# A transformer block in one program: the centre merged in place, LN1's variance and power for two groups at once, seven transposed buffers

## The chip, the core and the metric

The kernel runs on one core of a Trainium2 chip. The metric is the device time of one execution in microseconds. Before the change it is 3923.73 us, the median of three runs (3923.47 to 3927.55).

The core's engines each work through their own list of instructions in order, and wait for each other by semaphores. PE (TensorE) does matrix products and transposes, with PEld as its weight loads; DVE (VectorE), ACT (ScalarE) and POOL (GpSimd) do elementwise work; SP (SyncE) issues DMAs. POOL issues DMAs too, among them those that add to what is in the target. SBUF is the memory beside the engines, PSUM the one that PE writes to. In both, a tile is 128 partitions by so many elements.

## The reference

x has the shape (16, 128, 96, 96): 16 images, 128 channels, 96 x 96 pixels, in float32. For each image the reference computes

```
xn1 = layernorm over channels of x                       # LN1
q, k, v = xn1 wq^T, xn1 wk^T, xn1 wv^T                   # 8 heads of 16 channels
a = softmax(l2norm(q) l2norm(k)^T / 4)                   # over channels: one 16 x 16 matrix a head
x = x + (a v) wp^T
xn2 = layernorm over channels of x                       # LN2
h1 = w_in xn2                                            # 128 -> 512 channels
h2 = depthwise 3 x 3 convolution of h1 (w_dw)            # zero padding
x = x + w_out gelu(h2)                                   # 512 -> 128 channels
```

The attention is over channels, so all that it needs of the pixels is the Gram matrix of xn1. It is turned into one 128 x 128 matrix an image, which is then applied to xn1.

## The kernel before, in words

**Tiles.** An image is cut into 8 bands of 12 rows (1152 pixels), a band into 3 units of 4 rows (384 pixels). The 512 hidden channels are 4 chunks of 128. A tile of activations has channels on its partitions and pixels along the free axis. For layer norms the pixels go on the partitions: a *group* is 4 blocks of 128 pixels, transposed. An image has 18 groups.

**LN1** (`norm` with `second` false). For every group PE transposes x into a PSUM bank (`forth`, L1462), ACT copies it to a transposed buffer zT in SBUF (`copied`, L1499), DVE takes statistics of it in two instructions (`stats`, L1470), POOL forms variance plus epsilon (`variance`, L1475) and raises it to -1/2 (`power`, L1479), and POOL scales zT in place (`scaled`, L1503). Then PE adds the group to the Gram matrix (`gram`, L1510) and transposes it back (`back`, L1558), and ACT writes the result to the ring of normalised activations xn (`place`, L1564). There are 4 zT buffers. LN1 of an image runs while the image before it is in the feed-forward part. For image 0 nothing runs before it, and the scaling is done on DVE (L1483) straight from PSUM into other buffers.

**LN2** (`second` true). PE multiplies xn by the image's attention matrix (`mix`, L1412), ACT adds the bias (L1421), and a DMA from POOL adds x (L1424). Statistics, variance and power are as in LN1, but PE then only spreads the inverse deviations over the channels (L1558), and DVE multiplies (`place`, L1562) into the same ring xn.

**Feed-forward** (`conv_job`, one for a band and a chunk). PE computes h1 in pieces of 3 to 5 rows (`hidden`, L1756) and ACT copies them to a padded tile (`kept`, L1761). The nine taps of the convolution are divided among engines, scaled so that the centre tap has weight 1. ACT forms products for 2, 3 or 4 taps (`product`, L1772) into 8 buffers `pr`. POOL adds the first of these products and the unscaled centre into one common tile `merged` (`merge`, L1775; `merge_too`, L1778, adds a fourth product). DVE's first tap (L1784) reads `merged` and writes the accumulator in PSUM, further taps add to it (L1788), and the last one (L1784 again) writes h3. The second product, to which a third may have been added by a DMA (L1797), is added to h3 by an accumulating DMA (L1800), and ACT applies GELU (L1805). For some bands one chunk is computed by PE alone with nine products of the ring xn (`by_matmuls`, L1868). PE multiplies by w_out (L1904), DVE adds x (L1911), SP stores.

**The ring xn** has rows of 97 columns, of which 96 are used (`window`).

**Order.** The kernel is written with an explicit schedule. `Plan` holds every operation with an engine, an estimated duration, tokens it reads and writes, and a place. A simulation with these estimates gives each engine's list, and each list of buffers taken by several engines. `MOVES` then shifts single entries of these lists (entry number: by how much). The lists are fixed after that: each engine does its instructions in that order, whatever the real durations are. Semaphores follow from which tiles an instruction really reads and writes.

Of the kernel before, what the change touches and what calls it, by code (L numbers as in the profile page):

```python
# [17 lines left out]
UR = 4  # L18
# [18 lines left out]
QB = 1  # L37
H_BANKS = 4
TR_BANKS = 0
BK_BANKS = 0  # L40
# [6 lines left out]
ZT_BUFS = 4  # L47
BATCHES = 8
DIRECT = False
ENGINES = ("PE", "DVE", "ACT", "POOL", "SP")  # L50
IN_TURN = ("zT", "tr", "h3", "pr", "xb", "x1")
# [162 lines left out]
    PE={6: -1, 11: -1, 13: -1, 18: 0, 19: -3, 26: -1, 28: -1, 29: 7, 33: -3, 37: 3, 38: 6, 39: -4, 47: -2, 48: -2,  # L214
# [488 lines left out]
T_LAND = 1000  # L703
# [11 lines left out]
class Plan:  # L715
# [172 lines left out]
    def in_turn(self, lists):  # L888
# [40 lines left out]
        while len(sequence) < len(ops):  # L929
# [40 lines left out]
            if engine == "POOL":  # L970
                last_pool = None if queue else k
# [1017 lines left out]
```

## Time and profile before

| | before |
|---|---|
| median of 3 runs | 3923.73 us |
| profiled execution, its own time | 3923.85 us |
| its span in the profile | 3921.9 us |
| busy: PE, DVE, ACT, POOL | 3846.4, 3824.6, 3614.9, 3368.7 us |
| mean granted TensorE clock | 0.999 |

The span runs from the first to the last instruction of the profile; the execution's own time is 1.95 us longer. Rows of the profile name a line of the kernel, an engine, an operation, and the tile written and those read by their names in the program (`h` stands for the banks, the hidden tiles and h3 alike). Busy time of PE counts pipelined passes that overlap; an fp32 product is two passes. The waits name who waited for whom, with the sum in us, the number of times and the longest.

### The profile page before, as it was taken

What the parts mean: (1) busy time and instruction counts of PE and PEld (TensorE: products, weight loads), DVE (VectorE), ACT (ScalarE), POOL (GpSimd) and SP (SyncE); (2) the same over time, 40 slices, a digit from 0 to 9 for tenths busy, and PEclk for the clock granted to TensorE, in tenths of its full rate; (3) what the DMA queues carried; (4) which work ended last, traced back from release to release, by engine and by line L of the source; (5) the groups of instructions that cost most, each with busy time, mean ns of one, the idle gap of its engine ahead of it and who ended that gap; (6) DMA issues with size and microseconds to landing.
All of it is one profiled execution on the core that took longest, in us unless ns stands there. A gap on an engine that the chain in (4) does not pass through costs nothing.

```text
span 3921.9 us, 50494 instructions
## 1 busy us (share of the span) xinstructions
PE 3846.4 (98%) x16467; PEld 2477.5 (63%) x16467; DVE 3824.6 (98%) x4392; ACT 3614.9 (92%) x5478; POOL 3368.7 (86%) x3107
## 2 busy tenths in 40 slices
PE   8999999999999999999999999999999999999999
PEld 7666666666666666666666666666666666666555
DVE  7999999999999999999999999999999999999998
ACT  3999999999999999999999899999999999999986
POOL 5898899888898888989889899898998988888674
PEclk9999999999999999999999999999999999999999
DMA  3999999999999999999999999999999999999997
GB/s 93 188 205 205 191 211 205 201 203 195 214 197 209 204 192 212 203 206 203 202 206 202 195 211 203 207 197 210 207 205 201 205 208 195 207 202 188 202 188 150
DMA packets 191687, 777.36 MB, mean 198 GB/s; under 512 B 22208, under 2 KB 23616, under 8 KB 191424
## 3 DMA queue, kind: packets, MB, share of 16 engines
q0 software_dynamic: 151920, 622.33, 83.7%
q1 hardware_dynamic: 38784, 151.75, 10.6%
q8 instruction: 129, 2.11, 0.2%
q14 instruction: 134, 1.10, 0.1%
q10 hardware_dynamic: 720, 0.07, 0.0%
HBM read 148.85 MB, written 75.50 MB: 57 GB/s over the span
## 4 chain that ended last, share of the span: by engine, by line
PE 40%; DVE 9%; ACT 5%; DMA 3%; issue 2%; POOL 2%; POOLq 0%; DVEq 0%; ACTq 0%
PE h L1904 11%; PE h L1756 10%; PE h L1868 8%; DVE acc L1788 4%; PE h L1412 3%; PE h L1558 3%; PE g L1510 2%; PE h L1462 2%; ACT pr L1772 2%; DMA h<-pr 2%; DVE acc L1784 2%; DVE h L1784 1%; ACT h L1805 1%; DMA pr<-pr 1%; ACT h L1761 1%
## 5 line engine op out<-in xcount | busy, mean ns | idle before, releaser
L1772 ACT ACTIVATE pr<-h,ratio 128x1152 f32<-128x1152 f32 x1494 | 1845.2, 1268 | 14.2 <-DMA pr<-pr 2.7
L1788 DVE SCALAR_TENSOR_TENSOR acc<-h,ratio,acc 128x1152 f32<-128x1152 f32 (+1 forms) x1308 | 1810.1, 1384 | 10.9
L1775 POOL TENSOR_TENSOR merged<-pr,h 128x1152 f32<-128x1152 f32 x466 | 1212.6, 2602 | 116.6 <-DVE acc L1784 56.1
L1756 PE MATMUL h<-xn,winT 128*128 128x384 f32 (+2 forms) x2802 | 1093.3, 496 | 17.9 <-ACT h L1761 5.5
L1904 PE MATMUL h<-h,woutT 128*128 128x384 f32 x3072 | 1098.6, 487 | 3.6 <-ACT h L1761 1.4
L1868 PE MATMUL h<-xn,comp 128*128 128x380 f32 (+2 forms) x2430 | 893.5, 483 | 1.6 <-DVE st_b L1470 0.8
L1904 PEld LDWEIGHTS h<-h,woutT 128*128 128x128 f32 x3072 | 563.8, 189 | 372.6 <-ACT h L1761 16.4
L1761 ACT COPY h<-h 128x384 f32<-128x384 f32 (+2 forms) x1401 | 654.4, 492 | 110.2 <-PE h L1756 104.3
L1756 PEld LDWEIGHTS h<-xn,winT 128*128 128x128 f32 x2802 | 495.7, 189 | 348.5 <-ACT h L1761 29.7
L1784 DVE SCALAR_TENSOR_TENSOR acc<-h,ratio,merged 128x1152 f32<-128x1152 f32 x466 | 678.2, 1455 | 10.6 <-POOL merged L1775 4.7
L1784 DVE SCALAR_TENSOR_TENSOR h<-h,ratio,acc 128x1152 f32<-128x1152 f32 x467 | 655.2, 1403 | 4.5
L1805 ACT ACTIVATE h<-h,ksum 128x1152 f32<-128x1152 f32 (+1 forms) x586 | 611.0, 1069 | 27.0 <-DMA h<-pr 26.1
L1800 POOL DMA_DIRECT2D h<-pr x466 | 477.1, 1032 | 165.1 <-DVE h L1784 18.5
L1868 PEld LDWEIGHTS h<-xn,comp 128*128 128x128 f32 x2430 | 431.4, 190 | 234.2 <-issue 16.0
L1797 POOL DMA_DIRECT2D pr<-pr x466 | 469.6, 1025 | 73.7 <-ACT pr L1772 50.9
L1479 POOL TENSOR_TENSOR ve_a<-ve_a,mhalf 128x4 f32<-128x4 f32 x288 | 356.7, 1241 | 10.9
L1479 POOL TENSOR_TENSOR ve_b<-ve_b,mhalf 128x4 f32<-128x4 f32 x288 | 339.8, 1195 | 10.0
L1503 POOL TENSOR_TENSOR zT<-zT,ve_a 128x512 f32<-128x512 f32 x270 | 339.5, 1260 | 7.0
L1462 PE MATMUL h<-ident,x 128*128 128x128 f32 x2244 | 320.9, 275 | 9.3 <-DVE st_b L1470 2.3
L1462 PEld LDWEIGHTS h<-ident,x 128*128 128x128 f32 x2244 | 263.8, 141 | 101.3 <-issue 38.9
L1412 PE MATMUL h<-xn,mwT 128*128 128x384 f32 x768 | 288.8, 491 | 8.2 <-ACT x L1421 3.5
L1510 PEld LDWEIGHTS g<-zT 128*128 128x128 f32 x2160 | 271.9, 191 | 36.5 <-issue 3.0
(187 smaller groups left out, 3858.7 us busy)
## 6 DMA issues: line engine op xcount, KB each, us to landing
pr<-pr POOLq DMA_DIRECT2D x466, 576.0 KB, 7.2
h<-pr POOLq DMA_DIRECT2D x466, 576.0 KB, 7.8
x<-in_x_dram SPq DMA_DIRECT2D x128, 576.0 KB, 6.8
out_dram<-x SPq DMA_DIRECT2D x127, 576.0 KB, 4.9
x<-in_x_dram POOLq DMA_DIRECT2D x123, 576.0 KB, 8.3
out_dram<-x SPq DMA_DIRECT2D x3, 192.0 KB, 1.9
h<-in_L_conv_w_in_dram SPq DMA_DIRECT2D x1, 256.0 KB, 3.4
h<-in_L_conv_w_out_dram SPq DMA_DIRECT2D x1, 256.0 KB, 3.6
```

The lines of the kernel that those rows point to most:

```text
L1462: nc.tensor.transpose(d["pT", q][:, k, :], xt[:, j * P : (j + 1) * P], ident)
L1479: nc.gpsimd.tensor_tensor(rstd, rstd, mhalf, ALU.pow)
L1756: nc.tensor.matmul(rows(ph), lhsT=winT[:, n, :], rhs=window(xn, r0 + r, e - r, 1), start=True, stop=True)
L1761: nc.scalar.copy(window(h1_, r, e - r, 1), rows(d.pop(("ph", r))))
L1772: nc.scalar.activation(to, shifted(t), AF.Copy, scale=ratio[:, n, t : t + 1])
L1775: nc.gpsimd.tensor_tensor(merged, d["pr", dma_taps[0]], shifted(UNIT), ALU.add)
L1784: nc.vector.scalar_tensor_tensor(to, shifted(t), ratio[:, n, t : t + 1], also, ALU.mult, ALU.add)
L1788: nc.vector.scalar_tensor_tensor(to, shifted(t)[:, lo:hi, cut], ratio[:, n, t : t + 1], to, ALU.mult, ALU.add)
L1800: nc.gpsimd.dma_start(out=h3_of(g, n), in_=d["pr", dma_taps[1]], accum_op=ALU.add)
L1805: nc.scalar.activation(h3, h3, AF.Gelu, bias=ksum[:, z, n : n + 1])
L1868: nc.tensor.matmul(d["pc"][:, lo:hi, cut], lhsT=comp[:, t, :], rhs=window(xn, r0 + dy, UR, dx)[:, lo:hi, cut], start=(t == order[0]), stop ...
L1904: nc.tensor.matmul(rows(d["po"]), lhsT=woutT[:, n, :], rhs=h3s[g, n][:, s * UR : (s + 1) * UR, :], start=(k == 0), stop=(k == NCH - 1),)
```

## The change

1. `merge` and `merge_too` write into the buffer of the first product instead of the common tile `merged`, which is dropped. The first tap reads that buffer.
2. LN1 of images 1 to 15 takes variance and power of two groups in one instruction each (`QA = 2`): the statistics of both groups go into one tile, and both groups' scalings come behind that power. Image 0 (`QB_0`) and LN2 (`QB`) stay at one group.
3. There are 7 zT buffers instead of 4.
4. The ring xn has rows of 96 columns, without the spare one. Rows are then read and written as one run; the nine products of `by_matmuls` cut their columns out of it as before.
5. Estimates in the planner are altered (PE's rate, small POOL operations, a lag behind a DMA issue on POOL), a place's turn for buffers no longer contains its shift, options that were off are removed, and the lists in `MOVES` are rewritten, with lists for the buffers `x1` and `xb` besides.

```diff
-QB = 1
+QA, QB, QB_0 = 2, 1, 1
-ZT_BUFS = 4
+ZT_BUFS = 7
...
-IN_TURN = ("zT", "tr", "h3", "pr", "xb", "x1")
+IN_TURN = ("zT", "h3", "pr", "xb", "x1")
...
 MOVES = dict(
-    PE={6: -1, 11: -1, 13: -1, 18: 0, 19: -3,
...
+    PE={3: 0, 5: -5, 10: -1, 11: 2, 16: -1, 19: -2,
...
-PE_RATE, SPARE = 0.989, 75
+PE_RATE, SPARE, LAG, ISSUED = 1.013, 75, 300, 250
...
-T_POWER = 360 + 165 * QT * QB
-T_SMALL = 190
+T_POWER = 360, 165
+T_SMALL = 275
...
-    xn = pad.tile([P, (RING + 2) * WP + 2], F32, name="xn")
+    xn = pad.tile([P, (RING + 2) * W], F32, name="xn")
...
-    merged = h1p.tile([P, BR, W], F32, name="merged")
...
+    def pixels(r, n):
+        return xn[:, r * W : (r + n) * W]
+
+    def xn_rows(r, lo, hi, dx, cut):
+        return rows(pixels(r + lo, hi - lo))[:, :, cut.start + dx - 1 : cut.stop + dx - 1]
...
-        return window(xn, ring_of(i, u * UR) + 1, UR, 1)
+        return pixels(ring_of(i, u * UR) + 1, UR)
...
-        return Place(place + (AT[of] + SHIFTS.get(max(0, int(place // STRETCH)), {}).get(of, 0)), RANK.get(kind, 0))
+        shift = SHIFTS.get(max(0, int(place // STRETCH)), {}).get(of, 0)
+        return Place(place + AT[of], shift + RANK.get(kind, 0))
...
+        qb = (QB if second else QA) if i else QB_0
...
-                    d["st"] = small.tile([P, QB * QT // 2, 6], F32, tag="st", name=f"st_{name}_{m}")
+                    d["st"] = small.tile([P, qb * QT // 2, 6], F32, tag="st", name=f"st_{name}_{m}")
...
-                ve = d["ve"] = small.tile([P, QB * QT], F32, tag="ve", name=f"ve_{name}_{m}")
+                ve = d["ve"] = small.tile([P, qb * QT], F32, tag="ve", name=f"ve_{name}_{m}")
...
-                nc.gpsimd.tensor_tensor(rstd, rstd, mhalf, ALU.pow)
+                nc.gpsimd.tensor_tensor(rstd, rstd, mhalf[:, : qb * QT], ALU.pow)
...
-                nc.gpsimd.tensor_tensor(z, z, d["rstd"].unsqueeze(2).to_broadcast([P, QT, P]), ALU.mult)
+                nc.gpsimd.tensor_tensor(z, z, d["rstd"][:, q % qb * QT : (q % qb + 1) * QT].unsqueeze(2).to_broadcast([P, QT, P]), ALU.mult)
...
-                    nc.vector.tensor_tensor(interior(i, u), rows(x_unit(xbs, i, u)), rows(d["pB"]), ALU.mult)
+                    nc.vector.tensor_tensor(interior(i, u), x_unit(xbs, i, u), d["pB"], ALU.mult)
...
-                rows(ph), lhsT=winT[:, n, :], rhs=window(xn, r0 + r, e - r, 1), start=True, stop=True
+                rows(ph), lhsT=winT[:, n, :], rhs=rows(pixels(r0 + r, e - r)), start=True, stop=True
...
-            nc.gpsimd.tensor_tensor(merged, d["pr", dma_taps[0]], shifted(UNIT), ALU.add)
+            to = d["pr", dma_taps[0]]
+            nc.gpsimd.tensor_tensor(to, to, shifted(UNIT), ALU.add)
...
-            nc.gpsimd.tensor_tensor(merged, merged, d["pr", dma_taps[3]], ALU.add)
+            to = d["pr", dma_taps[0]]
+            nc.gpsimd.tensor_tensor(to, to, d["pr", dma_taps[3]], ALU.add)
...
-                also = acc if t == left[-1] else merged if dma_taps else shifted(UNIT)
+                also = acc if t == left[-1] else d["pr", dma_taps[0]] if dma_taps else shifted(UNIT)
...
-            pool(T_MERGE, at("merge", j), merge, [*h1, pr[0]], [("merged", 0)], True)
+            pool(T_MERGE, at("merge", j), merge, h1, [pr[0], ("merged", 0)], True)
...
-            r = [*h1, ("merged", 0)] if k == 0 and dma_taps else h1
+            r = [*h1, pr[0], ("merged", 0)] if k == 0 and dma_taps else h1
```

More of the change, by code (lines that the diff above doesn't have):

```diff
@@ L706, with __new__ @@
 class Place(float):
-    def __new__(cls, turn, rank):
-        place = float.__new__(cls, turn + rank)
+    def __new__(cls, turn, late):
+        place = float.__new__(cls, turn + late)
         place.turn = turn
@@ L971, in in_turn @@
                 last_pool = None if queue else k
+                lag = 2 if queue else lag if time < free_at["POOL"] + 40 else 0
+                if queue:
+                    ns -= ISSUED
+                elif lag:
+                    result += LAG * lag / 2
+                    lag -= 1
             begin[k], done[k], own[k], free_at[engine] = time, time + result, time + mine, time + ns
@@ L1042, in tile_restormer_block @@
     banks = [p_h.tile([P, 4 * P], F32, name=f"h_{k}") for k in range(H_BANKS)]
-    trs_ = [p_h.tile([P, 4 * P], F32, name=f"tr_{k}") for k in range(TR_BANKS)]
-    bks = [p_h.tile([P, 4 * P], F32, name=f"bk_{k}") for k in range(BK_BANKS)]
     acc_banks = p_acc.tile([P, ACC_BANKS * 4 * P], F32, name="acc")
@@ L1057, in tile_restormer_block @@
     nc.gpsimd.memset(ones, 1.0)
-    mhalf = const.tile([P, QB * QT], F32, name="mhalf")
+    mhalf = const.tile([P, max(QA, QB) * QT], F32, name="mhalf")
     nc.gpsimd.memset(mhalf, -0.5)
@@ L1165, in t_mm @@
     def t_mm(n):
-        return 2 * max(111, 0.849 * n)
+        return 2 * max(110, 0.841 * n)
     def t_dve(n):
@@ L1411, in mix @@
                 pm = d["pm"] = bank((name, u), UT)
-                nc.tensor.matmul(rows(pm), lhsT=mats[i][0], rhs=interior(i, u), start=True, stop=True)
+                nc.tensor.matmul(rows(pm), lhsT=mats[i][0], rhs=rows(interior(i, u)), start=True, stop=True)
                 if (i, b) not in xbs:
@@ L1436, in x2, with batch @@
                 add(at("add_x", s, u), add_x, [], xb)
-        def pixels(s, m):
+        def batch(s, m):
             d = {}
-            qs = range(m * QB, (m + 1) * QB)
+            qs = range(m * qb, (m + 1) * qb)
             early = i == 0 and (not second or m < EARLY)
-            key_ = "h" if not TR_BANKS else "tr"
             def tr_of(q):
-                return ("acc", q % BANKS_0) if in_acc(q) else (key_, (name, q, "tr"))
+                return ("acc", q % BANKS_0) if in_acc(q) else ("h", (name, q, "tr"))
             def in_acc(q):
@@ L1450, in pixels @@
             apart = i == 0 and not second
-            from_psum = second or DIRECT or apart
+            from_psum = second or apart
             def forth(q):
@@ L1456, in forth @@
                 else:
-                    of = bank((name, q, "tr")) if key_ == "h" else trs_[plan.slot["tr", (name, q, "tr")]]
+                    of = bank((name, q, "tr"))
                 d["pT", q] = of.rearrange("p (t c) -> p t c", c=P)
@@ L1524, in pixels @@
                     to = [tr] if second or apart else [tr, both[0]]
-                    pe(112 * QT, at("forth" + ab, s, m * QB * QT // TPU), lambda q=q: forth(q), [xtok(u) for u in units], to)
+                    pe(110 * QT, at("forth" + ab, s, m * qb * QT // TPU), lambda q=q: forth(q), [xtok(u) for u in units], to)
                     continue
-                pe(112 * QT, at("forth" + ab, s, m * QB * QT // TPU), lambda q=q: forth(q), [xtok(u) for u in units], [tr, both[0]])
-                act(t_copy(QT * P), at("copied" + ab, s, m * QB * QT // TPU), lambda q=q: copied(q), [tr], both)
-            for j in range(QB * QT // 2):
+                pe(110 * QT, at("forth" + ab, s, m * qb * QT // TPU), lambda q=q: forth(q), [xtok(u) for u in units], [tr, both[0]])
+                act(t_copy(QT * P), at("copied" + ab, s, m * qb * QT // TPU), lambda q=q: copied(q), [tr], both)
+            for j in range(qb * QT // 2):
                 of = trs[2 * j // QT] if from_psum else (*zt_of(qs[2 * j // QT]), 0)
-                dve(341, at("stats" + ab, s, m * QB * QT // TPU), lambda j=j: stats(j), [of], [bt])
-            pool(T_SMALL, at("variance" + ab, s, m * QB * QT // TPU), variance, [], [bt])
-            pool(T_POWER, at("power" + ab, s, m * QB * QT // TPU), power, [], [bt])
+                dve(341, at("stats" + ab, s, m * qb * QT // TPU), lambda j=j: stats(j), [of], [bt])
+            pool(T_SMALL, at("variance" + ab, s, m * qb * QT // TPU), variance, [], [bt])
+            pool(T_POWER[0] + T_POWER[1] * qb * QT, at("power" + ab, s, m * qb * QT // TPU), power, [], [bt])
             for h, q in enumerate(qs if not second else ()):
@@ L1550, in back @@
             def back():
-                d["pB"] = bks[plan.slot["bk", (name, u)]][:, :UT] if BK_BANKS else bank((name, u, "back"), UT)
+                d["pB"] = bank((name, u, "back"), UT)
                 for j in range(TPU):
@@ L1561, in place @@
                 if second:
-                    nc.vector.tensor_tensor(interior(i, u), rows(x_unit(xbs, i, u)), rows(d["pB"]), ALU.mult)
+                    nc.vector.tensor_tensor(interior(i, u), x_unit(xbs, i, u), d["pB"], ALU.mult)
                 else:
-                    nc.scalar.copy(interior(i, u), rows(d["pB"]))
+                    nc.scalar.copy(interior(i, u), d["pB"])
             def place_row(r, row):
-                nc.scalar.copy(window(xn, r, 1, 1), interior(i, u)[:, row : row + 1, :])
+                nc.scalar.copy(pixels(r, 1), interior(i, u)[:, row * W : (row + 1) * W])
             copies = []
@@ L1574, in channels @@
                 copies.append((0, UR - 1, -1))
-            pb = ("bk", (name, u)) if BK_BANKS else ("h", (name, u, "back"))
+            pb = ("h", (name, u, "back"))
             quads = {(u * TPU + j) // QT: None for j in range(TPU)}
             if second:
-                ms = {q // QB: None for q in quads}
-                pe(112 * TPU, at("back" + ab, s, u), back, [("batch", (name, m)) for m in ms], [pb])
+                ms = {q // qb: None for q in quads}
+                pe(110 * TPU, at("back" + ab, s, u), back, [("batch", (name, m)) for m in ms], [pb])
                 dve(t_dve(UT), at("place" + ab, s, u), place, [pb, xtok(u)], [z_unit(i, u)])
             else:
-                pe(112 * TPU, at("back" + ab, s, u), back, [(*zt_of(q), k) for q in quads for k in range(2)], [pb, z_unit(i, u)])
+                pe(110 * TPU, at("back" + ab, s, u), back, [(*zt_of(q), k) for q in quads for k in range(2)], [pb, z_unit(i, u)])
                 act(t_copy(UT), at("place" + ab, s, u), place, [pb], [z_unit(i, u)])
@@ L1594, in norm @@
         u = 0
-        for m in range(NU * TPU // (QB * QT)):
-            pixels(place_of(m * QB * QT), m)
-            while u < NU and (u + 1) * TPU <= (m + 1) * QB * QT:
+        for m in range(NU * TPU // (qb * QT)):
+            batch(place_of(m * qb * QT), m)
+            while u < NU and (u + 1) * TPU <= (m + 1) * qb * QT:
                 channels(place_of(u * TPU), u)
@@ L1833, in conv_job @@
         if dma_taps:
-            pool(T_MERGE, at("merge", j), merge, [*h1, pr[0]], [("merged", 0)], True)
+            pool(T_MERGE, at("merge", j), merge, h1, [pr[0], ("merged", 0)], True)
             if len(dma_taps) > 3:
-                pool(T_MERGE, at("merge", j), merge_too, [pr[3]], [("merged", 0)], True)
+                pool(T_MERGE, at("merge", j), merge_too, pr[3:], [pr[0], ("merged", 0)], True)
         for k, t in enumerate(left):
-            r = [*h1, ("merged", 0)] if k == 0 and dma_taps else h1
+            r = [*h1, pr[0], ("merged", 0)] if k == 0 and dma_taps else h1
             w = all_acc if k < len(left) - 1 else h3
@@ L1868, in product @@
             nc.tensor.matmul(
-                d["pc"][:, lo:hi, cut], lhsT=comp[:, t, :], rhs=window(xn, r0 + dy, UR, dx)[:, lo:hi, cut],
+                d["pc"][:, lo:hi, cut], lhsT=comp[:, t, :], rhs=xn_rows(r0 + dy, lo, hi, dx, cut),
                 start=(t == order[0]), stop=(t == order[-1]),
```

40 lines of the change are left out of this document (20 added, 20 removed), and 1589 rows, old and new, of tables (ACT, DVE, PE, POOL).

## The prediction

> **What bounds the kernel now.** I read the page first, for busy shares and for the chain of work that ended last.
>
> ```profile
> span 3921.9 us, 50494 instructions
> ...
> PE 3846.4 (98%) x16467; PEld 2477.5 (63%) x16467; DVE 3824.6 (98%) x4392; ACT 3614.9 (92%) x5478; POOL 3368.7 (86%) x3107
> ...
> PE 40%; DVE 9%; ACT 5%; DMA 3%; issue 2%; POOL 2%; POOLq 0%; DVEq 0%; ACTq 0%
> PE h L1904 11%; PE h L1756 10%; PE h L1868 8%; DVE acc L1788 4%; PE h L1412 3%; PE h L1558 3%; PE g L1510 2%; PE h L1462 2%; ACT pr L1772 2%; DMA h<-pr 2%; DVE acc L1784 2%; DVE h L1784 1%; ACT h L1805 1%; DMA pr<-pr 1%; ACT h L1761 1%
> ```
>
> PE and DVE stand at 98% together, and the chain passes between them. PE's 98% is soft: its busy time counts overlapped passes. DVE's is hard, since its instructions barely overlap. So the second view is busy time by stage.
>
> ```profile
> 0.00:100.00 100.00, 89.97 (x582) 72.50 (x583) 72.02 (x187) 34.48 (x70) 55.88 (x112) 1.00 0.32 93
> 100.00:3880.00 3780.00, 3718.09 (x15767) 2382.37 (x15767) 3726.91 (x4183) 3563.19 (x5377) 3307.80 (x2992) 1.00 0.97 202
> 3880.00:3922.00 42.00, 38.33 (x122) 22.63 (x120) 25.70 (x24) 17.25 (x33) 5.06 (x4) 0.99 0.47 111
> ```
>
> The columns after the length are PE, PEld, DVE, ACT and POOL. Between 100 and 3880 us DVE is idle for 3780 - 3726.9 = 53 us (1.4%), ACT for 217 us and POOL for 472 us. The start and the end leave DVE idle for 28 and 16 us. The DMA engines are at 0.97 there, but the change neither adds nor removes a transfer, so they can't be relieved by it. This sets the scale: if the change shortens no DVE instruction, what it can win in the long stage is those 53 us. The third view is what DVE waits for in that stage.
>
> ```profile
> DVE x L1911 <- PE h L1904: 6.2, 13, 1.4
> DVE xn L1562 <- PE h L1558: 5.5, 11, 1.1
> DVE st_b L1470 <- PE h L1462: 4.3, 9, 1.1
> DVE acc L1784 <- POOL merged L1778: 3.7, 7, 1.2
> DVE acc L1784 <- POOL merged L1775: 3.3, 7, 1.4
> ```
>
> PE's three rows make 16 us, the merges on POOL 7 us. Nothing else is above 2.5 us. A lighter POOL by itself can therefore give back 7 us through DVE and no more.
>
> **The merge in place.** L1775 and L1778 wrote one common buffer, so the next merge had to wait until the first tap (L1784) had read it. Now each merge writes the product's own buffer, and that wait is gone.
>
> ```profile
> POOL merged L1775 <- DVE acc L1784: 56.1, 64, 2.7
> POOL merged L1775 <- ACT pr L1772: 48.6, 48, 5.1
> ```
>
> That is 56 us of POOL idle, out of 472, on an engine that has room. What is late next is the product on ACT (48.6 us already). What queues behind a merge on POOL are the variances, the powers and the issues of the accumulating DMAs. I credit no POOL time as such, only the 7 us for which DVE waited for merges; bounds 0 and -7, and I take **-7**, because the merges lose both this wait and the work below from ahead of them. The price is that the first product's buffer stays taken until the tap has read it, not until the merge is done. There are eight such buffers, and ACT waited for a merge to free one for very little:
>
> ```profile
>   POOL merged L1775: 2.2, 5
> ```
>
> A buffer freed one tap later costs ACT at most that again and a little more, and the 217 us of ACT idle cover it: **0**. If that cover is gone, each late product makes its accumulating DMA, and then its GELU, late by a tap, 1.4 us.
>
> The wait had also kept something apart. A merge and a first tap both read two operands from SBUF, and they don't run side by side:
>
> ```profile
> L1784 DVE SCALAR_TENSOR_TENSOR acc<-h,ratio,merged x466: 1396/1412/3682, 87.8 to 3884.7; 128x1152 f32<-128x1152 f32 x156
> ```
>
> ```profile
> 1746.96 2.63 POOL L1503 TENSOR_TENSOR zT<-zT,ve_a 128x512 f32<-128x512 f32 x2
> ...
> 1747.14 3.68 DVE L1784 SCALAR_TENSOR_TENSOR acc<-h,ratio,merged 128x1152 f32<-128x1152 f32 x1
> ```
>
> The tap that met two scalings in a row took 3.68 us where the median is 1.41. With a mean of 1455 ns (its row stands below), all such blocking costs 466 x (1.455 - 1.412) = 20 us now. Without the old wait, a merge whose product is there could begin ahead of the preceding tap and hold it up. I went through the 64 waits in the order of time: in nine of them POOL came free before that tap had begun. First, one in the middle with its tap, and last:
>
> ```profile
> 714.16 2.43 POOL L1775 TENSOR_TENSOR merged<-pr,h 128x1152 f32<-128x1152 f32 x1 [2.21 <-DVE acc L1784]
> ...
> 1757.20 1.41 DVE L1784 SCALAR_TENSOR_TENSOR acc<-h,ratio,merged 128x1152 f32<-128x1152 f32 x1
> 1758.76 2.42 POOL L1775 TENSOR_TENSOR merged<-pr,h 128x1152 f32<-128x1152 f32 x1 [2.23 <-DVE acc L1784]
> ...
> 3794.17 2.42 POOL L1775 TENSOR_TENSOR merged<-pr,h 128x1152 f32<-128x1152 f32 x1 [2.70 <-DVE acc L1784]
> ```
>
> In the middle one POOL was free at 1758.76 - 2.23 = 1756.53, the tap began at 1757.20. A merge begun at 1756.53 would end at 1758.95 and push the tap by 1.75 us. Over the nine that makes 9 x 1.75 = 16 us, if every product had been there. In the other 55 the tap was already running, and the merge would wait for it as before. I take **+3**, some two cases, since the work ahead of the merges moves too; the bounds are -20 (all blocking gone) and +16.
>
> [...]
>
> **Variance and power for two groups at once.** For images 1 to 15 that is 15 x 18 / 2 = 135 pairs; image 0 and LN2 stay at one group.
>
> ```profile
> L1479 POOL TENSOR_TENSOR ve_a<-ve_a,mhalf x288: 997/1032/2935, 8.5 to 3570.0; 128x4 f32<-128x4 f32 x144
> ...
> L1679 POOL TENSOR_TENSOR rn<-n,mhalf x16: 707/710/713, 54.2 to 3592.9; 128x2 f32<-128x2 f32 x16
> ...
> L1475 POOL TENSOR_SCALAR ve_a<-st_a x288: 184/396/2281, 8.2 to 3567.0; 128x4 f32<-128x4 f32 x144
> ```
>
> The power of eight columns isn't in the trace. Two and four columns give (1032 - 710) / 2 = 161 ns a column, so eight take an estimated 1032 + 4 x 161 = 1676 ns against 2 x 1032: 0.39 us less a pair. One variance less saves up to 0.40 us. Together 135 x 0.79 = 106 us of POOL, which comes to nothing directly: POOL's 472 idle us hide it, and its share in the merges is in the -7.
>
> Against it stands a longer way for the first group of a pair. Its scaling (L1503), Gram matmuls (L1510) and transposes back (L1558) now wait for the second group's statistics, and PE has other passes queued behind them. The trace shows how near that wait is today:
>
> ```profile
> PEld h L1558 <- POOL zT L1503: 5.2, 11, 1.3
> ...
> PEld g L1510 <- POOL zT L1503: 1.9, 4, 0.8
> ```
>
> So 270 scalings made PE wait 7 us, and LN1 of an image runs a whole image ahead of its use. Seven transposed buffers in place of four hold the two to three more groups under way. I take **0**. The bounds are -7 (these waits go) and +20: one in ten of the 135 pairs late by the whole 1.68 us power makes 135 / 10 x 1.68 = 23, less some that is covered.
>
> **The activations without a padding column.** The diff also stores xn with 96 columns a row, not 97. Matmuls that read whole rows then read one run of 384. The trace has both kinds of reading:
>
> ```profile
> L1904 PE MATMUL h<-h,woutT 128*128 128x384 f32 x3072 | 1098.6, 487 | 3.6 <-ACT h L1761 1.4 <-DVE st_b L1470 1.2 <-DVE xn L1562 0.6
> L1756 PE MATMUL h<-xn,winT 128*128 128x384 f32 x2184 | 849.4, 492 | 12.9 <-ACT h L1761 3.2 <-DVE x L1911 2.4 <-ACT xn L1564 2.0
> L1784 DVE SCALAR_TENSOR_TENSOR acc<-h,ratio,merged 128x1152 f32<-128x1152 f32 x466 | 678.2, 1455 | 10.6 <-POOL merged L1775 4.7 <-POOL merged L1778 3.7
> L1868 PE MATMUL h<-xn,comp 128*128 128x384 f32 x788 | 322.4, 491 | 1.6 <-DVE st_b L1470 0.8 <-ACT h L1761 0.5
> L1412 PE MATMUL h<-xn,mwT 128*128 128x384 f32 x768 | 288.8, 491 | 8.2 <-ACT x L1421 3.5 <-DVE st_b L1470 3.2 <-ACT d L1720 0.5
> ...
> L1911 DVE TENSOR_TENSOR x<-h,x 128x384 f32<-128x384 f32 x384 | 210.5, 550 | 20.3 <-PE h L1904 18.8 <-ACT h L1752 0.7 <-ACT h L1805 0.3
> L1562 DVE TENSOR_TENSOR xn<-x,h 128x384 f32<-128x384 f32 x384 | 209.9, 548 | 11.1 <-PE h L1558 5.5 <-issue 2.4 <-ACT x L1421 1.5
> ```
>
> L1904 reads 384 in one run at 487 ns; the reads of xn in rows take 4 to 5 ns more. So PE saves 2184 x 5 + 788 x 4 + 768 x 4 = 17 us. How much of that is on the path follows from the chain, where a run of passes shows their true pace, and from the group of all L1756:
>
> ```profile
> 3904.79 13.56 PE h L1904 x42
> ...
> L1756 PE MATMUL h<-xn,winT 128*128 128x384 f32 (+2 forms) x2802 | 1093.3, 496 | 17.9 <-ACT h L1761 5.5
> ```
>
> A pass takes 13.56 / 42 = 323 ns, so L1756's 10% of the chain, 392 us, is 1214 of its 2802 passes, 43%. 17 x 0.43 gives **-7**; bounds 0 and -17. On DVE the write to xn gains nothing: 548 ns with the padding against 550 for L1911, which writes one run.
>
> **The order lists.** Every engine's list of moves is rewritten along with these edits. I can't cost this from a row; where it goes wrong is a rival. For image 0, at the start, the work is the same: 0, within 10 us either way, out of DVE's 28 idle us there.
>
> **The sum.** -7 + 3 + 0 - 7 = -11 us. The profiled execution took 3923.85 us (1.95 us outside its span), the median of the runs is 3923.73: 3923.85 - 11 = 3912.9, and 3913 against that median is -0.3%. A measurement of this kernel tells about 0.2%, 8 us, from no change.
>
> **The rivals.**
>
> *Hidden anyway.* DVE's busy time stays at 3825 us, and the gaps that PE and POOL no longer cause are filled by the next wait in line. For it: no DVE instruction gets shorter, and the chain's changes of engine are frequent. Against it: DVE's waits are named and two of the changes bear on them. Time: 3923, within 8 us.
>
> [...] At the first tap, POOL's two-operand instructions start ahead of it more often: merges without the old wait, and scalings that now come in pairs, as in the row at 1746.96, where the price was 3.68 - 1.41 = 2.27 us. For it: the nine cases, and 135 pairs released by one power. Against it: only some 20 of 466 taps are held up today. The other terms make -14 us, so from 14 / 2.27, some six more taps than today, it eats the gain. All nine merges (16 us) and eight taps met by a pair (18 us) give 3923.85 - 14 + 34 = 3944.
>
> *The order doesn't fit the pairs.* PE comes to Gram or back passes ahead of the pair's scalings, and everything behind on PE waits. If 20 pairs hit that for 1.68 us and DVE follows, 34 - 11 = +23: 3947. Against it: 7 us of such waits today.
>
> *More than the terms.* The new order also closes half of DVE's idle time in the long stage, 53 us less the 7 that are in the sum: 3923.85 - 11 - 23 = 3890.
>
> **How the numbers follow.** Forecast 0.43, hidden anyway 0.23, ports 0.12, order 0.14, more 0.08. Faster by over 0.2%: three quarters of the forecast's 0.43 (its term for PE may stay hidden), a tenth of the second and the last case: 0.32 + 0.02 + 0.08 = 0.42. Slower: the two slow cases but for a sixth, and 0.03 of the second: 0.22 + 0.03 = 0.25. The rest, 0.33, is no change. The forecast's own range is 3900 to 3923. For 8 times in 10 the low end takes in the better order, 3890, and the high end both slow ones, 3948.
>
> **What would show it.** Right: the wait of the merge for the tap (56.1 us) gone; the waits of DVE for merges near 0; the power with eight columns near 1.68 us, 135 of them; L1756 at 487 ns; DVE's busy time within 5 us of 3825. Wrong: first taps with a mean well above 1455 ns (ports), PE waiting for zT by more than 20 us (order), or DVE's busy time down by more than 10 us, which no term here gives.

## The result and the profile after

The changed kernel takes 3964.95 us (median of four runs, 3961.66 to 3970.0) against 3924.68 us for the kernel before, measured beside it: a ratio of 1.0103, with a 95% interval of 1.0085 to 1.012. It is 40 us slower. The prediction had 3913, with a range of 3890 to 3948.

The profiled execution took 3970.0 us, the longest of the four. First its page: the span, the busy times and the shares of the chain that ended last.

```profile
span 3968.2 us, 49765 instructions
...
PE 3856.2 (97%) x16467; PEld 2490.3 (63%) x16467; DVE 3861.1 (97%) x4392; ACT 3617.0 (91%) x5478; POOL 3295.3 (83%) x2840
...
PE 31%; DVE 9%; ACT 4%; DMA 4%; POOL 2%; issue 2%; DVEq 0%; POOLq 0%; ACTq 0%
```

POOL has become 73 us lighter (3368.7 before), as the pairs were meant to make it; 106 us were forecast. But DVE has become 36.5 us busier (3824.6 before) with the same 4392 instructions. Its idle time, span less busy, went only from 97.3 to 107.1 us. Of the 46.3 us between the two spans, 36.5 lie inside DVE's instructions and 9.8 in the waits between them. The group rows say which instructions. Columns: count, busy time and mean ns of one, idle time before them and what ended it.

```profile
L2457 DVE SCALAR_TENSOR_TENSOR acc<-h,ratio,pr 128x1152 f32<-128x1152 f32 x466 | 714.1, 1532 | 5.9 <-POOL pr L2451 2.7 <-POOL pr L2447 2.0
L2447 POOL TENSOR_TENSOR pr<-pr,h 128x1152 f32<-128x1152 f32 x466 | 1270.7, 2727 | 66.5 <-ACT pr L2443 65.7
```

The first taps took 678.2 us before and 714.1 now: 35.9 of the 36.5 us. The wait of the merge for the tap (56.1 us before) is gone, and the merges themselves went from a mean of 2602 ns to 2727.

DVE's waits in the whole span, with us in total, times and the longest:

```profile
DVE x L2584 <- PE h L2577: 20.6, 17, 4.3
DVE xn L2233 <- PE h L2229: 18.7, 29, 2.6
...
DVE acc L2457 <- POOL pr L2451: 2.7, 3, 1.1
DVE acc L2457 <- POOL pr L2447: 2.0, 6, 0.5
```

DVE waits 4.7 us for merges, against 4.7 + 3.7 = 8.4 us before in the same view. Its wait in LN2 for PE's spreading of the inverse deviations (L2229; 5.5 us before) is 18.7.

What a long tap looks like is seen in the timeline (start, length, engine, line; in brackets the idle time before it). This one is the longest of the trace:

```profile
778.55 0.92 POOL L2470 DMA_DIRECT2D pr<-pr  x1
778.67 7.45 DVE L2457 SCALAR_TENSOR_TENSOR acc<-h,ratio,pr 128x1152 f32<-128x1152 f32 x1
...
779.23 1.32 POOL L2174 TENSOR_TENSOR zT<-zT,ve_a 128x512 f32<-128x512 f32 x1
780.24 0.47 POOL L2146 TENSOR_SCALAR ve_b<-st_b 128x4 f32<-128x4 f32 x1
780.38 1.17 POOL L2473 DMA_DIRECT2D h<-pr  x1
780.98 1.47 POOL L2470 DMA_DIRECT2D pr<-pr  x1
781.54 3.35 POOL L2447 TENSOR_TENSOR pr<-pr,h 128x1152 f32<-128x1152 f32 x1
783.92 3.06 POOL L2150 TENSOR_TENSOR ve_b<-ve_b,mhalf 128x4 f32<-128x4 f32 x1
786.04 0.54 DVE L2233 TENSOR_TENSOR xn<-x,h 128x384 f32<-128x384 f32 x1
...
786.63 0.90 PE L2229 MATMUL h<-ident,ve_b 128*128 128x128 f32 x3 [5.56 <-DVE xn L2233]
```

The median of the first taps was 1.41 us before. This one was held for 6 us by a scaling, a variance and the next merge, which passed it, with two DMA issues between them. The old wait made that merge impossible: it would have stood behind the tap. The power behind the merge took 3.06 us instead of 1.0 and ended at 786.98, 0.86 us after the tap, which fits a wait for the tap. PE stood still for 5.6 us meanwhile. The windows show what followed; the columns after the length are PE, PEld, DVE, ACT, POOL, granted clock, DMA share, GB/s.

```profile
781.00:786.60 5.60, 0.08 (x1) 0.00 (x0) 5.60 (x3) 1.84 (x2) 5.60 (x4) 0.78 1.07 262
786.60:791.00 4.40, 4.37 (x13) 3.17 (x14) 4.40 (x6) 0.85 (x3) 0.39 (x1) 0.50 0.95 189
791.00:800.00 9.00, 9.00 (x46) 6.22 (x46) 8.20 (x11) 8.16 (x13) 3.99 (x5) 1.00 0.42 82
```

After the gap PE ran at half its clock. In the whole trace eleven first taps took over 3.6 us (one before). From 150 us to 10 us before the end, nine stretches at half clock add up to 47.8 us. The kernel before has none there, but two just ahead, at 105 and 119 us, of 3.4 us each. Stretches at half clock are counted between these bounds from here on.

Last, the rows for the pairs: the powers (minimum, median and maximum ns), PE's waits for a scaling, and ACT's waits for a product buffer.

```profile
L2150 POOL TENSOR_TENSOR ve_a<-ve_a,mhalf x153: 1006/1662/3092, 10.5 to 3609.1; 128x8 f32<-128x8 f32 x135, 128x4 f32<-128x4 f32 x18
```

```profile
PEld g L2181 <- POOL zT L2174: 3.7, 7, 0.9
...
PE g L2181 <- POOL zT L2174: 0.5, 2, 0.3
```

```profile
ACT pr L2443 <- DMA h<-pr: 8.0, 10, 2.5
ACT pr L2443 <- DMA pr<-pr: 6.9, 9, 2.1
ACT pr L2443 <- DVE acc L2457: 3.0, 1, 3.0
```

A power of eight columns takes 1.66 us. PE's wait for scalings at the Gram matmuls is 4.2 us, and 0.8 at the transposes back, so the pairs' order fits. ACT waits 18.6 us for buffers with the smaller rows, where it was 5.5.

### The profile page after: what moved, and what is told of

Its sections match the earlier page's. It is cut to its first block, busy times and chain, and to the rows that moved or that the text cites. A ratio compares the mean times of both kernels' runs of the same rounds, so it can differ in the third digit from the quotient of the medians.

```text
span 3968.2 us, 49765 instructions
## 1 busy us (share of the span) xinstructions
PE 3856.2 (97%) x16467; PEld 2490.3 (63%) x16467; DVE 3861.1 (97%) x4392; ACT 3617.0 (91%) x5478; POOL 3295.3 (83%) x2840
## 4 chain that ended last, share of the span: by engine, by line
PE 31%; DVE 9%; ACT 4%; DMA 4%; POOL 2%; issue 2%; DVEq 0%; POOLq 0%; ACTq 0%
PE h L2577 9%; PE h L2427 8%; PE h L2541 7%; DVE acc L2461 4%; DMA h<-pr 2%; PE h L2084 2%; PE g L2181 2%; DVE acc L2457 2%; PE h L2229 2%; PE h L2133 2%; ACT pr L2443 2%; DVE h L2457 2%; ACT h L2478 1%; POOL pr L2447 1%; DMA pr<-pr 1%
## 5 line engine op out<-in xcount | busy, mean ns | idle before, releaser
L2447 POOL TENSOR_TENSOR pr<-pr,h 128x1152 f32<-128x1152 f32 x466 | 1270.7, 2727 | 66.5 <-ACT pr L2443 65.7
L2427 PE MATMUL h<-xn,winT 128*128 128x384 f32 (+2 forms) x2802 | 1112.7, 498 | 27.3 <-DVE xn L2233 7.1
L2577 PE MATMUL h<-h,woutT 128*128 128x384 f32 x3072 | 1123.0, 488 | 7.1 <-DVE x L2584 2.0
L2457 DVE SCALAR_TENSOR_TENSOR acc<-h,ratio,pr 128x1152 f32<-128x1152 f32 x466 | 714.1, 1532 | 5.9 <-POOL pr L2451 2.7
L2473 POOL DMA_DIRECT2D h<-pr x466 | 459.6, 988 | 283.5 <-PE h L2577 49.4
L2133 PE MATMUL h<-ident,x 128*128 128x128 f32 x2244 | 337.3, 277 | 27.1 <-DMA x<-in_x_dram 8.2
L2150 POOL TENSOR_TENSOR ve_b<-ve_b,mhalf 128x4 f32<-128x4 f32 x288 | 349.3, 1230 | 9.3
L2174 POOL TENSOR_TENSOR zT<-zT,ve_a 128x512 f32<-128x512 f32 x270 | 352.6, 1338 | 2.9
L2084 PE MATMUL h<-xn,mwT 128*128 128x384 f32 x768 | 302.5, 494 | 15.7 <-ACT x L2093 6.0
L2181 PE MATMUL g<-zT 128*128 128x129 f32 x2160 | 286.3, 276 | 0.5 <-POOL zT L2174 0.5
```

Source lines behind the costliest of these rows:

```text
L2133: nc.tensor.transpose(d["pT", q][:, k, :], xt[:, j * P : (j + 1) * P], ident)
L2181: nc.tensor.matmul(grams[i][:, : P + 1], lhsT=zt[:, :P], rhs=zt, start=(q == 0 and k == 0), stop=(q == NU * TPU // QT - 1 and k == QT - 1),)
L2427: nc.tensor.matmul(rows(ph), lhsT=winT[:, n, :], rhs=rows(pixels(r0 + r, e - r)), start=True, stop=True)
L2447: nc.gpsimd.tensor_tensor(to, to, shifted(UNIT), ALU.add)
L2457: nc.vector.scalar_tensor_tensor(to, shifted(t), ratio[:, n, t : t + 1], also, ALU.mult, ALU.add)
L2577: nc.tensor.matmul(rows(d["po"]), lhsT=woutT[:, n, :], rhs=h3s[g, n][:, s * UR : (s + 1) * UR, :], start=(k == 0), stop=(k == NCH - 1),)
```

## The experiments

The leading theory was that without the old wait merges start ahead of the previous first tap and hold it up. The rivals: the loss lies in the new order, in the pairs, or in the product buffers held one tap longer. Each edit keeps the order that its base kernel gives to every engine (the added repetitions and split instructions stand where the single ones stood). In code, "..." stands for lines that are left out. Medians in us, ratios against the kernel before measured beside it:

| kernel | median us (runs) | ratio [95%] |
|---|---|---|
| after_wait | 3928.59 (10) | 1.0009 [0.9998, 1.002] |
| before_inplace | 4047.18 (4) | 1.0311 [1.0296, 1.0327] |
| before_inplace_wait | 3963.15 (4) | 1.0092 [1.0079, 1.0106] |
| before_ring96 | 3921.12 (10) | 0.9993 [0.9984, 1.0003] |
| after_split | 3995.84 (4) | 1.0183 [1.0168, 1.0198] |
| after_wait_split | 3949.01 (4) | 1.0058 [1.0045, 1.0072] |
| before_lump | 4076.13 (4) | 1.0377 [1.0361, 1.0393] |
| before_spread | 4034.51 (4) | 1.0275 [1.0261, 1.0289] |
| after_gate | 3938.74 (5) | 1.003 [1.0017, 1.0044] |
| after_wait_gate | 3923.91 (11) | 0.9991 [0.9982, 1.0] |
| before_gate | 3916.23 (7) | 0.9976 [0.9965, 0.9987] |
| ring96_gate | 3914.25 (8) | 0.9972 [0.9961, 0.9982] |

### The wait put back into the changed kernel

The merge stays in place, and waits for the first tap ahead of it:

```
-            nc.gpsimd.tensor_tensor(to, to, shifted(UNIT), ALU.add)
+            m = nc.gpsimd.tensor_tensor(to, to, shifted(UNIT), ALU.add)
+            if first_tap:
+                tc.add_manual_dep(m.ins, first_tap[-1].ins.name, ...)
...
+                if t == left[0]:
+                    first_tap.append(v)      # v: the tap on DVE
...
```

> The changed kernel with one thing put back: each merge waits again until the first tap of the job before it has ended (an explicit dependency; the merge still writes in place, every engine's order is the same). Theory A, the missing wait: merges that start ahead of a held-up first tap cost the 41 us. Then the first taps above 3.6 us go, their mean falls from 1532 ns to about 1455, half-clock stretches of PE in the middle of the run fall from 9 to 0 or 1, and the time is 3915 to 3930. Theory B, the order: the other order of the lists costs the 41 us by itself. Then the taps get shorter but the time stays above 3950. Theory C, pairs of scalings on POOL in a row hold up the taps: the mean of the first taps stays above 1490 ns and the time is 3940 to 3960.

The page, the tap's group and the merge's wait for it:

```profile
span 3932.5 us, 50062 instructions
...
PE 3841.3 (98%) x16467; PEld 2479.9 (63%) x16467; DVE 3826.6 (97%) x4392; ACT 3615.6 (92%) x5478; POOL 3276.8 (83%) x2840
```

```profile
L2459 DVE SCALAR_TENSOR_TENSOR acc<-h,ratio,pr 128x1152 f32<-128x1152 f32 x466 | 681.3, 1462 | 5.9 <-POOL pr L2453 2.8 <-POOL pr L2447 2.0
```

```profile
POOL pr L2447 <- DVE acc L2459: 46.5, 71, 3.4
```

One wait on POOL takes the median from 3964.95 to 3928.59, 36 of the 40 us. In the spans it is 35.7 us, and the first taps give 714.1 - 681.3 = 32.8 of them. DVE's idle time is 105.9 us against 107.1, so it hardly changed. The half clock fell from 47.8 to 13.7 us along with it, in three stretches where none or one had been expected, but the idle times show that it was a companion of the loss and not its size. The 4 us that are left can't be told from nothing: the interval of the ratio holds 1.

### The merge in place alone, and with its wait

In the kernel before, only the merge is put in place, with the product's buffer kept until the tap has read it; then the same dependency is added.

```
-            nc.gpsimd.tensor_tensor(merged, d["pr", dma_taps[0]], shifted(UNIT), ALU.add)
+            to = d["pr", dma_taps[0]]
+            nc.gpsimd.tensor_tensor(to, to, shifted(UNIT), ALU.add)
...
```

> The kernel before with the merge in place alone; every engine's order is that of before, the buffers of the first product are held until the tap has read them. Theory A: slower, since the nine merges that POOL could start early now do so, and those behind a held-up tap as well: first taps of 4 us and more appear, mean above 1480 ns, time 3935 to 3965, with half-clock stretches. Theory B: within 8 us of before, 3917 to 3932. The term of the prediction for it alone: -7 + 3 = -4, 3920.

> The kernel before with the merge in place, and each merge waiting for the first tap before it as the common tile had made it wait; the order of before. Theory A (the missing wait alone costs the 123 us of the merge in place): 3917 to 3932, no first tap above 4 us. Rival (the first product's buffers, held until the tap has read them, hold up ACT): it stays well above 3960, with ACT waiting for the tap at the products.

Without the wait, the page, the tap and ACT's waits:

```profile
PE 3886.8 (96%) x16467; PEld 2495.6 (62%) x16467; DVE 3911.3 (97%) x4392; ACT 3619.2 (89%) x5478; POOL 3385.5 (84%) x3107
```

```profile
L1788 DVE SCALAR_TENSOR_TENSOR acc<-h,ratio,pr 128x1152 f32<-128x1152 f32 x466 | 759.8, 1631 | 8.9 <-POOL pr L1778 3.8 <-POOL pr L1782 3.0
```

```profile
ACT pr L1774 <- DVE acc L1788: 36.4, 22, 5.7
ACT pr L1774 <- DMA pr<-pr: 23.0, 22, 3.1
ACT pr L1774 <- DMA h<-pr: 21.7, 22, 2.9
```

With it:

```profile
PE 3857.7 (97%) x16467; PEld 2479.3 (63%) x16467; DVE 3832.0 (97%) x4392; ACT 3617.7 (91%) x5478; POOL 3369.6 (85%) x3107
```

```profile
L1790 DVE SCALAR_TENSOR_TENSOR acc<-h,ratio,pr 128x1152 f32<-128x1152 f32 x466 | 679.4, 1458 | 9.5 <-POOL pr L1778 3.8 <-POOL pr L1784 3.3
```

```profile
ACT pr L1774 <- DMA h<-pr: 27.7, 28, 3.9
ACT pr L1774 <- DMA pr<-pr: 26.0, 24, 3.8
```

In the old order the edit by itself costs 123 us, three times what the whole change costs; the expectation had ended at 3965 us. The wait is worth 4047.18 - 3963.15 = 84 us. In the spans (4045.4 and 3965.1 us) it is 80.3, and the first taps give 759.8 - 679.4 = 80.4: all of it. Some 36 us stay when the taps are as short as before (0.0092 of 3924). In the profiled executions, 43 us apart, 36 are DVE's idle time, 133.1 us against 97.3. What the edit still changes is that the buffer stays held, and ACT's waits for a product buffer, some 65 us with the smaller rows against 5.5, are its trace. Only 4.6 us of them are waits for the tap itself; most are for the DMAs that read the other products. That held buffers are the cause is therefore argued from these waits and not shown; no run gave the kernel a ninth buffer.

### The pairs split again

Variance and power are done for each of the two groups in an instruction of its own, where the pair's stood; without and with the merges' wait.

```
...
-                nc.gpsimd.tensor_tensor(rstd, rstd, mhalf[:, : qb * QT], ALU.pow)
+                for k in range(0, qb * QT, QT):
+                    nc.gpsimd.tensor_tensor(rstd[:, k : k + QT], rstd[:, k : k + QT], mhalf[:, :QT], ALU.pow)
```

> The changed kernel with variance and power of a pair as two instructions each of four columns, at the same place in the same order. POOL gets some 100 us of work back. If POOL's lighter load is worth something, the time rises above 3975; if it is covered, it stays within 8 us of 3965. Theory C (a power that releases two scalings at once): no gain, since the scalings still stand one behind the other.

> The changed kernel with the merges' wait, and variance and power of a pair as two instructions each. This prices the part of the change that takes two groups at once, once the missing wait is out of the picture. If a POOL lighter by some 100 us is covered, as the prediction had it: within 8 us of 3929. If it is worth as much as without the wait: 3960.

After_split's taps, then after_wait_split's busy times and its waits for merges:

```profile
L2459 DVE SCALAR_TENSOR_TENSOR acc<-h,ratio,pr 128x1152 f32<-128x1152 f32 x466 | 733.0, 1573 | 12.3 <-POOL pr L2449 6.4 <-POOL pr L2453 4.7
```

```profile
PE 3848.2 (97%) x16467; PEld 2482.2 (63%) x16467; DVE 3830.0 (97%) x4392; ACT 3617.0 (92%) x5478; POOL 3358.2 (85%) x3110
```

```profile
DVE acc L2461 <- POOL pr L2449: 7.3, 12, 1.9
...
DVE acc L2461 <- POOL pr L2455: 6.0, 8, 1.5
```

The pairs are a gain, not the loss: 3949.01 - 3928.59 = 20 us with the wait, and 3995.84 - 3964.95 = 31 us without. With the wait most of it is DVE's idle time (3948.1 - 3830.0 = 118.1 us against 105.9): DVE waits 13.3 us for merges where the pairs leave 4.8. Without the wait most of it is in the taps (733.0 against 714.1), which fits a longer row of POOL instructions holding them longer. The wait is worth 47 us here. The 20 us lie between the two values that had been expected, none and 31.

### The ring of 96 columns alone

```
-    xn = pad.tile([P, (RING + 2) * WP + 2], F32, name="xn")
+    xn = pad.tile([P, (RING + 2) * W], F32, name="xn")
...
```

> The kernel before with the ring of 96 columns alone, the same order. The term of the prediction: matmuls that read whole rows fall from 492 to 487 ns, and the time by 7 us, 3917. The rival, hidden: passes get shorter, the time stays within 4 us of before. A third: passes stay at 492 ns, since the row break was not what cost the 5 ns.

```profile
L1910 PE MATMUL h<-h,woutT 128*128 128x384 f32 x3072 | 1101.4, 488 | 3.7 <-ACT h L1767 1.5 <-DVE st_b L1476 1.0 <-DVE xn L1568 0.7
L1762 PE MATMUL h<-xn,winT 128*128 128x384 f32 x2184 | 849.1, 493 | 15.9 <-DVE x L1917 4.2 <-ACT h L1767 3.8 <-ACT xn L1570 2.1
```

The passes over whole rows take 493 ns with rows that lie end to end, and took 492 with the padding. The premise was wrong: the 5 ns against L1910's passes don't come from the padding. What they come from stays open. The time is 3 us lower, and the interval of the ratio, 0.9984 to 1.0003, holds 1.

### A stall in lumps or spread out

To price the half clock of PE that comes with long taps, the kernel before repeats a last tap (the same value is written again): seven times in every 30th job, 96 extra taps in 16 lumps, or twice in every fifth job, 94 extra.

```
+                for _ in range(7 if t == left[-1] and j % 30 == 15 else 1):    # before_lump
+                for _ in range(2 if t == left[-1] and j % 5 == 0 else 1):      # before_spread
...
```

> The kernel before with the last tap of a job done seven times instead of once in every 30th job: 96 further instructions of 1.40 us on DVE, in 16 lumps of 8.4 us (the same value is written again). If PE's clock falls to half behind a gap in its work, and this is worth something, half-clock stretches appear in most of the 16 places and the time rises by more than the 96 x 1.34 = 129 us that DVE needs for them: 4075 to 4110. [...]

> The same with single repetitions in every fifth job: 94 further instructions on DVE, none next to another. DVE sets the pace in the long stage, so nearly all of 94 x 1.34 = 126 us is added: 4035 to 4055, with no more than three half-clock stretches. Less, if DVE's gaps take up some.

Span and mean granted clock, lumps first:

```profile
core 0: 4075.7 us, clock 0.982
```

```profile
core 0: 4032.5 us, clock 0.998
```

Two taps more, and 41.6 us between the medians, or 2.6 us a lump. Both times lie at the low edge of what was expected, the second one 0.5 us below it. Behind every one of the 16 lumps PE ran at half clock; with one stretch more these add up to 139.9 us, and the spread taps leave two stretches, 6.8 us. So a lump costs some 2.6 us more than the same taps spread out, its stretch at half clock included; that a lump of 8 us is also absorbed worse by the buffers isn't separated from it.

### Scalings that wait for the tap

The scaling can hold a tap as a merge does: the tap at 1747.14 in the kernel before took 3.68 us, against a median of 1.41. Here each scaling waits for the first tap ahead of it in the program, in four kernels: the changed one with merges free (after_gate), the changed one with their wait (after_wait_gate), the one before (before_gate), and the one before with the ring of 96 (ring96_gate).

```
-                nc.gpsimd.tensor_tensor(z, z, d["rstd"]..., ALU.mult)
+                m = nc.gpsimd.tensor_tensor(z, z, d["rstd"]..., ALU.mult)
+                if first_tap:
+                    tc.add_manual_dep(m.ins, first_tap[-1].ins.name, ...)
```

> The changed kernel with the scalings waiting for the last first tap before them in the program, but the merges free, as the change has them. If a scaling ahead of the tap is what begins each long hold-up, and the merge only lengthens it: first taps above 3.6 us fall from 11 to 3 or fewer, time 3930 to 3945. If merges alone begin them, behind the issue of a DMA: half of the 11 stay, time above 3950.

> The changed kernel with the merges waiting for the first tap before them, and the scalings too; the order of the change. What is left of held-up taps there is 21 us. If the scalings cause it, as with the kernel before: mean of the first taps below 1435 ns, and 8 to 15 us less than with the merges' wait alone: 3913 to 3921. If pairs of scalings now come late for PE: no gain, and PE waiting for zT by more than 20 us.

> The kernel before with the scalings' wait alone, ring of 97 columns. If the gain of the ring and the wait together (0.9972) is the wait's: 3912 to 3918, ratio 0.997 to 0.9985. If it took both: above 3920.

> The kernel before with the ring of 96 columns, and with each scaling of LN1 on POOL waiting for the last first tap that stands before it in the program. What holds up the 19 taps above 1.5 us are such scalings; where tap and scaling stand in that order, the tap now goes first. If most do: the mean of the first taps falls from 1453 to below 1430 ns, and the time by 5 to 15 us against the ring alone, 3906 to 3916. If the scalings stand before the taps in the program: no change, 3921.

Before_gate's first taps; then ring96_gate's busy times, its first taps, and the price of the wait on POOL:

```profile
L1786 DVE SCALAR_TENSOR_TENSOR acc<-h,ratio,merged 128x1152 f32<-128x1152 f32 x466 | 666.2, 1430 | 10.7 <-POOL merged L1777 5.1 <-POOL merged L1780 3.2
```

```profile
PE 3839.5 (98%) x16467; PEld 2488.2 (64%) x16467; DVE 3808.8 (97%) x4392; ACT 3613.1 (92%) x5478; POOL 3358.1 (86%) x3107
```

```profile
L1792 DVE SCALAR_TENSOR_TENSOR acc<-h,ratio,merged 128x1152 f32<-128x1152 f32 x466 | 664.2, 1425 | 11.9 <-POOL merged L1783 5.9 <-POOL merged L1786 3.5
```

```profile
POOL zT L1509 <- DVE acc L1792: 16.9, 28, 1.4
```

With merges free, waiting scalings win back 26 of the 36 us (3964.95 to 3938.74), and five of the eleven long taps remain, which is neither of the two outcomes that were expected: it fits hold-ups that begin with either kind of POOL work, and six of the eleven are gone where scalings can't begin one. With both waits the changed kernel is at 3923.91, no different from the kernel before, with a mean of the first taps of 1440 ns; both just miss what was expected. In the kernel before, the scalings' wait alone gives a ratio of 0.9976: the blocking that was there all along, 20 us by the prediction's count, goes down to 466 x (1.430 - 1.416) = 6.5 us (the tap's mean and median in before_gate). Ring96_gate has the lowest median of all, 3914.25 us, ratio 0.9972 with an interval of 0.9961 to 0.9982: 0.3% below the kernel before, at a price of 17 us of idle time on POOL. Whether the ring adds to the wait isn't told: the two intervals overlap.

## Why the prediction was wrong

**The missing wait (+3): the right mechanism, the size wrong.** This is the step that failed. It measured +36 us in the changed kernel, and +84 in the old order. That is 33 of the 52 us between forecast and result. The prediction named the mechanism and took two of nine cases, at most 16 us; its rival of taps held up more often, with a chance of 0.12, reached 34 us with 17 blocked taps, and put the time at 3944. (By the trace the cases are eight, 14 us: in the others POOL came free at least 0.1 us after the tap had begun.) The cases were found by walking through the trace of before and asking where POOL stood free ahead of the tap. But that trace was made under the wait: POOL was paced by it. Without it POOL runs ahead: merges recorded as starting more than 0.1 us before the previous tap had ended number 113 in the changed kernel and 103 in before_inplace, none where the wait is. Those that began over 1.5 us before its end are few (12 and 27). And blocking isn't one instruction for one tap: a tap that a scaling holds is passed by the next merge, as at 778.67, for 6 us instead of 2.3. The row at 1746.96 already had this in it: the tap began 0.18 us into the first of two scalings, and was held through the second one as well. The price of a case was wrong as well as the number.

The prediction's count let a merge hold a tap until its own end and no longer, 1.75 us in its example. The full block fits the trace of the changed kernel, and goes both ways: the tap at 778.67 ended 1.2 us after the merge that had passed it, and the power of 3.06 us ended 0.86 us after the tap that it met. But this tap was held for 6 us, through several POOL instructions, so here the measurement decides. What lies behind the block, which the prediction's list of chances calls "ports", no run shows.

**DVE's busy time.** The prediction said that more than 5 us from 3825 would speak against it, and named first taps well above 1455 ns as the sign of taps held up. 3861.1 us and 1532 ns are that sign. That DVE's instructions barely overlap was read too strictly: in the trace of before their lengths add up to 4136.7 us against 3824.6 busy. The scale of 53 us that it set held only if no DVE instruction grew longer, and the first taps did.

**The held product buffers (0): wrong in the old order.** They cost some 36 us there if the reading above is right; that ACT's 217 us of idle time cover it compared totals, where the buffer would be missed at a few places that stand on the path. In the changed order ACT waits only 18.6 us for buffers, and what that costs is not separated.

**Variance and power in pairs (0 directly): wrong.** Worth 20 us with the wait. The 106 us of POOL, 80 as measured (3375.5 us busy in after_split against 3295.3), were called hidden by 472 us of POOL's idle time. Idle time elsewhere didn't hide work that stands ahead of the merges: DVE's waits for them are 13.3 us with the powers split and 4.8 without. The estimate of the power (1676 ns) was right: 1.66 us measured. This price was taken in the changed order, in which the split powers stand at one place; it doesn't hold for before's order without more.

**The merges' waits (-7).** DVE's waits for merges fell by 3.7 us, not by 7, and it is mainly the pairs that brought them down: with the pairs split they are at 13.3 us (after_wait_split), and the merge in place alone takes them only from 8.4 to 6.8 (before_inplace). No run shows a gain from the merge in place.

**The ring (-7).** The passes didn't get shorter; the -3 us measured can't be told from nothing.

**The order.** The rival in which PE comes to the Gram or back passes too early is refuted: 4.2 and 0.8 us. But the order isn't free. After_wait has the new order, the held buffers, the pairs and the ring, and stands 4 us above before. With -20 for the pairs and -3 for the ring, held buffers and order together cost about 27 us, worked out and not shown; after_wait_split, 23 us above before, is the same sum without the pairs. How it splits between the two stays open.

## What to carry to other kernels

A wait that only protects a buffer can also pace an engine (worth 36 us here in the new order, 84 in the old): look at what the waiting instruction would overtake before you remove it, and don't count the cases in a trace that was made under the wait. Where two engines block each other, check the busy time of the one that sets the end: here 35.9 us of stalls were inside DVE's first taps, where no view of waits shows them, and its idle time grew by 9.8. An explicit dependency between them can be cheaper than the overlap it forbids (46.5 us of POOL's waiting took 36 us off the time), and the merge in place would need one.

## What the hardware showed beyond that

**Taps seem to be held by POOL instructions ahead of their recorded start.** Counted over six of the traces (before, after, after_wait, before_inplace, before_ring96, after_split; 2796 first taps, held meaning longer than 1.55 us): of 113 taps that began while POOL was issuing a DMA and had a scaling or a merge recorded as starting up to 0.7 us later, 59 were held. Of 33 where POOL was idle or on a small instruction ahead of it, 2. Of 900 during a DMA issue with no scaling or merge within 1 us, one. So a POOL instruction queued behind a DMA issue seems to hold up the tap before its recorded start; that is read from the counts, and no run tests it. The tap at 778.67 is of this kind: it began 0.56 us ahead of the scaling's record.

**PE's clock can fall after short gaps.** In the changed kernel the nine stretches stand behind gaps of PE of 1.8 to 5.6 us. One behind a gap of 2.2 us:

```profile
2462.77 0.32 PE L2229 MATMUL h<-ident,ve_b 128*128 128x128 f32 x1 [2.21 <-POOL ve_b L2150]
```

```profile
2463.40:2467.00 3.60, 3.60 (x8) 1.89 (x7) 3.60 (x5) 0.55 (x1) 2.86 (x4) 0.53 0.98 256
```

The length of the gap alone doesn't decide. In the kernel before, the clock fell at 105 and at 119 us, behind gaps of at most 1.5 and 1.7 us; at 2166.37, behind a gap of 1.70 us, it stayed at 1.00. What else decides is open.

The stretches at half clock last 3.4 or 6.8 us each in the changed kernel. In before_lump the 17 stretches last 8.2 us in the mean (139.9 us), so some are longer.
